# A graph layer on one core: the products of a range's last 32 nodes turned over the four column strips of PE, and a wider spacing of later groups' rank products

## The chip, the cores and the metric

One core of one Trainium2 chip. The metric is the device time of one execution in microseconds. Three runs of the kernel before gave 538.83, 539.52 and 541.97 us; their median is 539.52.

## What is computed

There are 6250 nodes with 128 features and 100,000 edges sorted by destination. Every edge carries one of two messages of its source node, by the edge's type; each node adds up what it receives, adds an own term, and the result goes through relu, a residual and a layer norm.

```python
m_data = X[src] @ W_data.T + b_data
m_ctrl = X[src] @ W_control.T + b_control
msg = where(edge_type == 0, m_data, m_ctrl)
agg = segment_sum(msg, dst, num_segments=6250)
h = x + relu(agg + (x @ W_self.T + b_self))
out = (h - mean(h)) / sqrt(var(h) + 1e-5)
```

## The kernel before

**Tables.** PE first makes both messages of every node, split in three bf16 parts of 128 columns that together hold the fp32 value. They stay in SBUF as m3 (98 tables of 128 rows, 384 columns) and go to DRAM as table.

**Ranges and groups.** 39 ranges of 160 destination nodes (WN) follow, numbered from 0, in 11 groups of 1, 2 and then 4 ranges (GROUPS); group 4 is the fifth and holds ranges 11 to 14. The last few nodes are done at the end of the main part by gathers.

**Ranks.** For each group, `ranks` reads the edges (win), finds each edge's place in a short list by source table, and makes an index. Its steps run over several engines: one-hots of the source block (hots, DVE, L799 and L803), counts (PE, L810) that go out to DRAM and back as past (SP, L830 and L833), rank products (PE, L846, two at a time into the one PSUM buffer rk, each emptied by a DVE reduction to slot, L851), one-hots of the slots (hr and two, DVE, L875 and L881), scatter products (PE, L890), and the write of the result as packed (SP, L917). Edges that find no room in a list go through a second list (L993) and gathered rows gl.

**Sums.** For each range, `sums` loads packed back, broadcast over the partitions, as rows (SP, L1043; three buffers), turns it into a one-hot with a compare on DVE (L1053), and makes a second one-hot hot2 of the destinations in two or three compares (DVE, L1061). Then 25 steps g follow. Stage 1 (L1075) picks messages: four products of 32 output rows, one on each 32-column strip of PE, into a PSUM buffer (g with three buffers, every fourth step x with one). ACT, or DVE where the planner finds it earlier, copies that to SBUF as gs (L484, L485). Stage 2 adds them up by destination in a: four products of 384 columns for the first 128 nodes of the range (L1092), again one on each strip, and three of 128 columns for its last 32 nodes (L1095), one for each of the three bf16 parts, on strips 0, 1 and 2. Stage 2 of a step is put three steps behind stage 1. At the end bs takes the 96 x 128 sums of the last 32 nodes, and a product with fold (L615, a stack of three unit matrices of 32) adds the three parts.

**Order.** Nothing is executed where it is written: `add` hands the planner an instruction, or a list of engines to choose from, with a guessed duration and a due time. `Plan.run` walks through the program in its own time, takes on each engine the ready instruction with the earliest due time, and so writes one fixed order per engine. Due times of the ranks of a group come from the loop at L1191: `when` starts LEAD (80) ahead of the group's ranges, the rank products follow `late` behind it, `step` apart for each table k, and what follows them (scatter, packed, lists) is due behind the last. The planner counts 0.168 us for stage 1 and 0.178 for stage 2.

Of the kernel before, what the change touches and what calls it, by code (L numbers as in the profile page):

```python
# [10 lines left out]
F32 = mybir.dt.float32  # L11
# [5 lines left out]
SP = mybir.EngineType.SP  # L17
# [4 lines left out]
P = 128  # L22
D = 128
D3 = 3 * D
# [20 lines left out]
R = 32  # L45
W4 = WN - P
NT = 2 * NB
NS = 25
# [218 lines left out]
def sums_over_windows(ctx, tc, x, xt, edges, w, bias, out, total):  # L267
    nc = tc.nc
    V, A, G, T, S = nc.vector, nc.scalar, nc.gpsimd, nc.tensor, nc.sync
    dram = ctx.enter_context(tc.tile_pool(name="dram", bufs=1, space=DRAM))  # L270
    const = ctx.enter_context(tc.tile_pool(name="consts", bufs=1))
    work = ctx.enter_context(tc.tile_pool(name="work", bufs=2))
# [3 lines left out]
    add = plan.add  # L276
# [5 lines left out]
    def B(pool, shape, dtype, name, bufs=1, room=None):  # L282
        return Buf(plan, pool, shape, dtype, name, bufs, room)

    def C(shape, dtype, name):
        return Buf(plan, const, shape, dtype, name, 1)

    XC = 4 * WN
    T0 = 36.0
    DOUBLE = ('lo1', 'to1', 'slot2', 'pay', 'inside', 'unit')  # L290
    TW = 13.0
# [4 lines left out]
    AD = 0.45  # L296
    RP, RA, RS = 1, 14, 0.9
    GAP, LEAD, LF, SF = -12, 80, .3, .010


    r0 = C([125, RH, 1], I32, "r0")
# [22 lines left out]
    def vec(due, cols, fn, r, w, rate=1.04):  # L324
        return add("DVE", dve(cols, rate), fn, due, r, w)

    def vp(on_pool, due, cols, fn, r, w, rate=1.04, slow=1.0):
# [15 lines left out]
    ident = C([P, P], F32, "ident")  # L343
# [38 lines left out]
    later = C([P, 2 * R], BF16, "later")  # L382
    vec(2, R, lambda: V.memset(later.t[:, :R], 0.0), [], [(later, 0)], 0.3)
    vec(2, R, lambda: V.memset(later.t[:, R:], 1.0), [], [(later, 1)], 0.3)
    fold = C([3 * R, R], F32, "fold")
    vec(30, R, lambda: V.tensor_add(fold.t, ident.t[: 3 * R, 0:R], ident.t[: 3 * R, R : 2 * R]),
        [ident], [fold])
    vec(30, R, lambda: V.tensor_add(fold.t, fold.t, ident.t[: 3 * R, 2 * R : 3 * R]),
        [ident, fold], [fold])
    minus = C([P, P], BF16, "minus")  # L390
    vec(1.5, P, lambda: V.tensor_scalar_mul(minus.t, ident.t, -1.0), [ident], [minus])
    wbase = C([P, NW], I32, "wbase")
# [28 lines left out]
    def count_rows():  # L421
        for h in range(RH):
# [28 lines left out]
                                    start=True, stop=True), 0.8, [first_f, ident], [first_ps])  # L451
# [6 lines left out]
    def load_edges(b, n, out_, due, buf, key, engine, rows=P):  # L458
        def fn():
# [23 lines left out]
    evict = lambda o, src, cols, due, r, w, lat=0.0: add(  # L483
        [("ACT", act(cols), lambda: A.copy(o(), src())),  # L484
         ("DVE", dve(cols), lambda: V.tensor_copy(o(), src()))], None, None, due, r, w, lat)  # L485
# [14 lines left out]
    m3_key = lambda g: [(m3, (min(g, NS - 1), i)) for i in range(3)]  # L500
# [9 lines left out]
    for c, n in enumerate(XB):  # L510
        cuts = [0, 2, 4, 8, n] if c == 0 else [0, 4, 8, n]
# [15 lines left out]
    for q in range(NS):  # L527
        bs = range(2 * q, min(2 * q + 2, NB))
        nb = len(bs)
        due = 4.0 + MS * q  # L530
# [4 lines left out]
        key = (mp, half)  # L535
        mt = lambda mp=mp, half=half: mp.t[:, half] if len(mp.shape) == 3 else mp.t

        n = 2 * nb * D
        ts = slice(4 * q, 4 * q + 2 * nb)

        for i, b in enumerate(bs):
            c, k, xk = pieces[b]
# [173 lines left out]
    def ranks(gi, w0, nw, when, late, step, engines):  # L716
# [6 lines left out]
        n = nw * KT  # L723
# [62 lines left out]
        vt = low()  # L786
# [7 lines left out]
        for k0 in range(0, KT, ks):  # L794
            k1 = min(k0 + ks, KT)
            m = (k1 - k0) * nw
# [60 lines left out]
        for ci, (k0, k1) in enumerate(zip(cs, cs[1:])):  # L857
            dc = t0 + 1 + step * k1
            m = (k1 - k0) * nw
            c = slice(k0 * nw, k1 * nw)  # L860
            kw = lambda b: b.t.rearrange("p k w -> p (k w)")
            vec(dc, m, lambda c=c, kw=kw: V.tensor_tensor(
                kw(own_n)[:, c], kw(slot)[:, c], kw(unit)[:, c], op=ALU.mult),
                [(slot, k - k % per) for k in range(k0, k1)] + [unit], [(own_n, ci)])
            vec(dc, m, lambda c=c, kw=kw: V.tensor_single_scalar(
                kw(own_n)[:, c], kw(own_n)[:, c], 127, op=ALU.bitwise_and), [(own_n, ci)],
                [(own_n, ci)])
            vec(dc, 2 * m, lambda c=c: V.scalar_tensor_tensor(  # L868
                fl(slot2)[:, c], f2(own_n)[:, c], SLOT0, f2(inside)[:, c], op0=ALU.add,
                op1=ALU.mult), [(own_n, ci), inside], [(slot2, ci)])  # L870
            s4 = [EP, m, R // 2, 2]
            v4 = lambda ap: ap.rearrange("p m (c d) -> p m c d", d=2)
            hr = B(work, [EP, m, R], BF16, "hr", 1, 48 * R)
            two = B(work, [P, m, 2, R], BF16, "two", 1, 48 * 2 * R)
            vec(dc, m * R, lambda c=c, s4=s4, v4=v4, hr=hr: V.tensor_tensor(  # L875
                v4(hr.t),
                slots.t[:EP].rearrange("p (c d) -> p c d", d=2)[:, None].to_broadcast(s4),
                fl(slot2)[:, c, None, :].to_broadcast(s4), op=ALU.is_equal),
                [(slot2, ci), slots], [hr], 0.52)
            for i, f in enumerate((lo1, to1)):  # L880
                tf = lambda e, c=c, s4=s4, v4=v4, i=i, f=f, hr=hr, two=two: e.tensor_tensor(  # L881
                    v4(two.t[:EP, :, i, :]), v4(hr.t),
                    fl(f)[:, c, None, :].to_broadcast(s4), op=ALU.mult)
                vec(dc, m * R, lambda tf=tf: tf(V), [hr, f], [(two, i)], 0.52)

            def scatter(k0=k0, k1=k1, two=two):
                for k in range(k0, k1):
                    for i in range(nw):
                        q = 64 * (i % 2)
                        T.matmul(vv()[q : q + 64, i // 2, :],  # L890
                                 two.t[:EP, (k - k0) * nw + i].rearrange("p f r -> p (f r)"),
                                 ha()[:EP, k, i, :], start=k == 0 and i < 2, stop=k == KT - 1,
                                 skip_group_check=True)
            add("PE", .25 + m * 0.0275, scatter, dc + 1, [(two, 0), (two, 1)] + hkeys(k0, k1), [vt])
        d2 = t0 + 1.5 + step * KT
        vs = B(work, [P, nh, NT], BF16, "vs", 1, 2 * NT)
        both = nw // 2
# [131 lines left out]
        return to_d, gls  # L1029


    def sums(gi, w0, nw, placed):
        to_d, gls = placed
        xc = B(work, [D, nw * WN], F32, "xc", 2, XC)
# [3 lines left out]
        for i in range(nw):  # L1038
# [29 lines left out]
            for g in range(NS):  # L1068
                d = due + TW * g / NS
                gp = B(ps, [P, 512], F32, *(("g", 3) if gi < 2 or g % 4 < 3 else ("x", 1)))  # L1070
                last = g == NS - 1

                def stage1(g=g, gp=gp, sp=sp, last=last):
                    for t in range(2 if last else 4):
                        T.matmul(gp.t[R * t : R * t + R, :D3], sp.t[:, :, 4 * g + t],  # L1075
                                 m3.t[:, 4 * g + t, :], start=True, stop=True)
                s1.append(add("PE", 0.168, stage1, d, [sp] + m3_key(g), [gp]))
                lag = 2 if gi < 2 else 3
                if g >= lag:
                    s2[g - lag].after.append(s1[g])  # L1080
                if last:
                    gs = gls[i]
                    evict(lambda gs=gs: gs.t[:64], lambda gp=gp: gp.t[:64, :D3], D3, d + 0.3,
                          [gp], [(gs, "t")], LAT)
                else:
                    gs = B(work, [P, D3], BF16, "gs", 6)
                    evict(lambda gs=gs: gs.t, lambda gp=gp: gp.t[:, :D3], D3, d + 0.3, [gp], [gs],
                          LAT)

                def stage2(g=g, gs=gs, a=a, hot2=hot2, last=last):  # L1090
                    for j in range(4):
                        T.matmul(a.t[R * j : R * j + R, :D3], hot2.t[:, g, R * j : R * j + R],  # L1092
                                 gs.t, start=g == 0, stop=False, skip_group_check=True)
                    for c in range(3):
                        T.matmul(a.t[R * c : R * c + R, D3:], hot2.t[:, g, P:],  # L1095
                                 gs.t[:, c * D : (c + 1) * D], start=False, stop=last,
                                 skip_group_check=True)
                s2.append(add("PE", 0.178, stage2, d + 0.9, [gs, (hot2, sum(g >= c for c in cuts[1:-1]))], [a]))
                s2[-1].slack = .1
                if g == 12:  # L1100
                    def own_a(i=i, a=a, xc=xc):
                        own(lambda j, m: a.t[R * j : R * j + R, :D],
                            lambda j, m: xc.t[:, i * WN + R * j : i * WN + R * j + R], P)
                    add("PE", 0.28, own_a, d + 1, [xc, w_sb, one3, brows], [a])
            bs = B(work, [3 * R, D], F32, "bs", 5)
            evict(lambda bs=bs: bs.t, lambda a=a: a.t[: 3 * R, D3:], D, due + TW + 0.8, [a], [bs]).slack = 0.25
            got.append((w0 + i, a, due + TW + 0.8, bs))
        return got

# [81 lines left out]
    w0 = 0  # L1191
    todo = []
    for gi, nw in enumerate(GROUPS):
        if gi == 0:
            when, late, step, engines = 0.0, 12.0, 0.5, ["SP"]
        elif gi == 1:
            when, late, step, engines = 8.0, 14.0, 0.6, ["SP", "ACT"]
        else:
            span = nw * TW
            when = max(when + late + 22 * step + GAP, T0 + w0 * TW - LEAD)  # L1200
            late, step, engines = LF * span, SF * span, ["SP"]
        todo.append((gi, w0, nw, when, late, step, engines))
        w0 += nw
    placed = [ranks(*a) for a in todo]
# [169 lines left out]
```

## Time and profile before

| | us |
|---|---|
| median of three runs | 539.52 |
| the profiled execution | 542.22 |
| its span, first to last instruction | 540.4 |
| PE / DVE / ACT / POOL busy | 502.1 / 441.1 / 429.0 / 201.5 |
| first stage 1 product | 60.8 |
| chain of the end: share of PE | 40% |

A row of the timeline has the start, the length, the engine, the line, the operation, what it writes and reads, its size and how many were merged; the idle time ahead of it stands in brackets with what ended it. A row of the groups ends with busy time and mean nanoseconds of one, then the idle time ahead of them. [...] Matmuls of 32 columns each are on one of four strips; the profile doesn't name the strip.

### The profile page before, as it was taken

The numbers are of one execution on the slowest core, as the hardware profiler recorded it, in microseconds if no ns is written. First come the engines' busy times: TensorE is split into PE (matmuls) and PEld (weight loads), VectorE is DVE, ScalarE is ACT, GpSimd is POOL, SyncE is SP. The second block draws the span as 40 slices with busy tenths as digits, with TensorE's granted clock in tenths as the row PEclk, the third lists the DMA queues.
The fourth block names the chain that finished last, engine by engine and source line by source line (L and its number), as shares of the span: only waits on it lengthen the run. The fifth ranks groups of instructions, "written<-read, shape, count | busy, mean of one in ns | idle before, by whom it ended". The sixth has DMA issues, their size and how long they took to land. (4 is left out here: it accounts for less than half of the span.)

```text
span 540.4 us, 30907 instructions
## 1 busy us (share of the span) xinstructions
PE 502.1 (93%) x13288; PEld 432.6 (80%) x13288; DVE 441.1 (82%) x1168; ACT 429.0 (79%) x1077; POOL 201.5 (37%) x284
## 2 busy tenths in 40 slices
PE   7799879799999988999999999999999999999991
PEld 4465557699889877888988887888898899888990
DVE  6388989889989997898989889979978678956642
ACT  4566767698889877888988878978898898878990
POOL 1000535700830684176067247707701720542000
PEclk9989899999999998999999999999999999999997
DMA  7466661540453055325413533351342352234200
GB/s 244 160 256 224 240 181 29 167 161 6 134 145 88 12 139 151 98 77 152 141 38 111 141 95 95 91 180 41 115 128 88 115 163 89 63 107 126 70 19 17
DMA packets 44932, 63.43 MB, mean 117 GB/s; under 512 B 19178, under 2 KB 35279, under 8 KB 44751
## 3 DMA queue, kind: packets, MB, share of 16 engines
q1 hardware_dynamic: 41745, 56.22, 33.5%
q0 software_dynamic: 1120, 2.23, 2.0%
q10 hardware_dynamic: 1922, 2.91, 1.7%
q8 instruction: 106, 1.74, 1.3%
q14 instruction: 39, 0.32, 0.2%
HBM read 45.61 MB, written 13.82 MB: 110 GB/s over the span
## 5 line engine op out<-in xcount | busy, mean ns | idle before, releaser
L1092 PE MATMUL a<-gs,hot 128*32 128x384 bf16 x3744 | 376.1, 328 | 0.4 <-issue 0.3
L484 ACT CAST gs<-g 128x384 bf16<-128x384 f32 x700 | 302.9, 492 | 64.3 <-PE g L1075 53.6
L1075 PE MATMUL g<-m,rows 128*32 128x384 bf16 x2958 | 327.1, 336 | 9.0 <-DVE rows L1053 5.7
L1075 PEld LDWEIGHTS <-rows 128*32 128x32 bf16 x3822 | 253.4, 134 | 27.7 <-DVE rows L1053 6.5
L1095 PE MATMUL a<-gs,hot 128*32 128x128 bf16 x2808 | 273.1, 220 | 2.1 <-issue 2.1
L1092 PEld LDWEIGHTS <-hot 128*32 128x32 bf16 x3900 | 206.4, 98 | 6.7 <-issue 3.1
L1095 PEld LDWEIGHTS <-hot 128*32 128x32 bf16 x2925 | 155.6, 97 | 14.1 <-issue 2.4
L1075 PE MATMUL x<-m,rows 128*32 128x384 bf16 x864 | 122.0, 335 | 0.0
L484 ACT CAST gs<-x 128x384 bf16<-128x384 f32 x199 | 98.3, 494 | 8.6 <-PE x L1075 5.7
L1061 DVE TENSOR_TENSOR hot<-iota_b,to_d 128x1920 bf16<-128x1920 bf16 (+2 forms) x85 | 93.1, 1105 | 0.1
L851 DVE TENSOR_REDUCE slot<-rk 124x8 f32<-124x400 f32 (+2 forms) x99 | 56.1, 567 | 22.3 <-PE g L1075 10.3
L674 POOL TENSOR_SCALAR xr<-xr,mv,rstd 128x128 f32<-128x128 f32 (+1 forms) x44 | 56.5, 1289 | 21.9 <-DVE rstd L651 18.4
L846 PE MATMUL rk<-hots,tri 128*32 128x400 bf16 (+1 forms) x388 | 51.3, 337 | 4.5 <-DVE slot L851 1.5
L1053 DVE TENSOR_SCALAR rows<-rows,pid 128x3136 bf16<-128x3136 bf16 (+1 forms) x46 | 41.6, 904 | 5.7 <-DMA rows<-packed 5.7
L937 POOL TENSOR_SCALAR pv<-slot 124x88 f32<-124x88 bf16 x9 | 9.5, 1058 | 79.6 <-DVE slot L868 74.2
L624 DVE TENSOR_REDUCE s<-a 128x128 f32<-128x384 f32 (+1 forms) x40 | 22.1, 551 | 15.7 <-ACT bs L484 9.9
L1016 POOL DMA_INDIRECT sr<-table,at x20 | 29.8, 1489 | 10.8 <-DVE at L1004 6.2
L491 POOL COPY to_d<-vs 32x100 bf16<-32x100 bf16 (+1 forms) x72 | 29.2, 406 | 5.9 <-DVE vs L911 2.7
L846 PEld LDWEIGHTS <-tri 128*32 128x32 bf16 x428 | 22.9, 96 | 9.9 <-issue 8.6
L803 DVE TENSOR_TENSOR hots<-hots,val 124x1200 bf16<-124x1200 bf16 (+3 forms) x42 | 28.0, 675 | 0.0
L799 DVE TENSOR_TENSOR hots<-iota_b,st 124x1200 bf16<-124x1200 bf16 (+3 forms) x42 | 27.6, 671 | 0.0
L767 POOL TENSOR_SCALAR pay<-u 124x88 f32<-124x88 f32 x9 | 8.9, 994 | 46.2 <-DVE u L752 45.1
(224 smaller groups left out, 667.9 us busy)
## 6 DMA issues: line engine op xcount, KB each, us to landing
rows<-packed SPq DMA_DIRECT2D x36, 784.0 KB
table<-m SPq DMA_DIRECT2D x12, 768.0 KB
xc<-in_xt SPq DMA_DIRECT2D x9, 320.0 KB
rows<-packed ACTq DMA_DIRECT2D x3, 784.0 KB
rows<-in_xt SPq DMA_DIRECT2D x8, 256.0 KB
xr<-in_x SPq DMA_DIRECT2D x8, 256.0 KB
out<-xr SPq DMA_DIRECT2D x8, 256.0 KB
gl<-sr SPq DMA_DIRECT2D x39, 48.0 KB
```

The source lines that it names most:

```text
L484: [("ACT", act(cols), lambda: A.copy(o(), src())), ("DVE", dve(cols), lambda: V.tensor_copy(o(), src()))], None, None, due, r, w, lat)
L491: "POOL", 0.25 + cols * 0.0014, lambda: G.tensor_copy(o(), src()), due, r, w)
L674: fp = lambda k=k, m=m: G.tensor_scalar(h.t[:m, k, :], h.t[:m, k, :], mv.t[:m, k, 0:1], rstd.t[:m, k : k + 1], op0=ALU.subtract, op1=ALU.mult)
L803: vec(when + 2 + pace * k0, m * NC, lambda k0=k0, k1=k1, hs4=hs4, hp=hp: V.tensor_tensor(hp(), hp(), fl(val)[:, k0 * nw : k1 * nw, None, : ...
L846: T.matmul(acc.t[R * j : R * j + R, : (k1 - k0) * wide], tri.t[:, R * j : R * j + R], flat(k0, k1, P), start=True, stop=True, skip_group_c ...
L851: vec(due, (k1 - k0) * wide, lambda k0=k0, k1=k1, acc=acc: V.tensor_reduce(slot.t[:, k0:k1, :], acc.t[:EP, : (k1 - k0) * wide].rearrange(" ...
L1016: add("POOL", GC, lambda pr=pr, sr=sr: G.indirect_dma_start(out=sr.t[: room(pr)], out_offset=None, in_=table[:, :], in_offset=bass.Indirec ...
L1053: add("DVE", dve(half * NT, 0.305) + 0.05, lambda sp=sp, rs=rs: V.tensor_scalar(sp.t[:, rs], sp.t[:, rs], pid1.t, None, op0=ALU.is_equal), ...
L1061: lambda i=i, hot2=hot2, s4=s4, c0=c0, c1=c1: V.tensor_tensor(hot2.t[:, c0:c1].rearrange("p g (c d) -> p g c d", d=2), iota1_b.t.rearrange ...
L1075: T.matmul(gp.t[R * t : R * t + R, :D3], sp.t[:, :, 4 * g + t], m3.t[:, 4 * g + t, :], start=True, stop=True)
L1092: T.matmul(a.t[R * j : R * j + R, :D3], hot2.t[:, g, R * j : R * j + R], gs.t, start=g == 0, stop=False, skip_group_check=True)
L1095: T.matmul(a.t[R * c : R * c + R, D3:], hot2.t[:, g, P:], gs.t[:, c * D : (c + 1) * D], start=False, stop=last, skip_group_check=True)
```

## The change

```diff
+    LEAD4, SF4 = 90, .025
...
-    fold = C([3 * R, R], F32, "fold")
-    vec(30, R, lambda: V.tensor_add(fold.t, ident.t[: 3 * R, 0:R], ident.t[: 3 * R, R : 2 * R]),
+    fold = C([P, R], F32, "fold")
+    vec(30, R, lambda: V.tensor_add(fold.t, ident.t[:, 0:R], ident.t[:, R : 2 * R]),
...
+    for j in (2, 3):
+        vec(30, R, lambda j=j: V.tensor_add(fold.t, fold.t, ident.t[:, R * j : R * j + R]),
...
-            add("PE", .25 + m * 0.0275, scatter, dc + 1, [(two, 0), (two, 1)] + hkeys(k0, k1), [vt])
+            add("PE", .2 + m * 0.016, scatter, dc + 1, [(two, 0), (two, 1)] + hkeys(k0, k1), [vt])
...
+    load = [0] * 4
+
+    def turn(n, cols):
+
+        js = sorted(range(4), key=lambda j: (load[j], j))[:n]
+        for j in js:
+            load[j] += cols
+        return js
...
-                    for t in range(2 if last else 4):
+                    for t in (0, 1) if last else turn(4, D3):
...
-                s1.append(add("PE", 0.168, stage1, d, [sp] + m3_key(g), [gp]))
+                s1.append(add("PE", 0.163, stage1, d, [sp] + m3_key(g), [gp]))
...
-                    for j in range(4):
+                    for j in turn(4, D3):
...
-                    for c in range(3):
-                        T.matmul(a.t[R * c : R * c + R, D3:], hot2.t[:, g, P:],
-                                 gs.t[:, c * D : (c + 1) * D], start=False, stop=last,
+                    for c, j in enumerate(turn(3, D)):
+                        T.matmul(a.t[R * j : R * j + R, D3:], hot2.t[:, g, P:],
+                                 gs.t[:, c * D : (c + 1) * D], start=False, stop=g > NS - 3,
...
-                s2.append(add("PE", 0.178, stage2, d + 0.9, [gs, (hot2, sum(g >= c for c in cuts[1:-1]))], [a]))
+                s2.append(add("PE", 0.204, stage2, d + 0.9, [gs, (hot2, sum(g >= c for c in cuts[1:-1]))], [a]))
...
-            bs = B(work, [3 * R, D], F32, "bs", 5)
-            evict(lambda bs=bs: bs.t, lambda a=a: a.t[: 3 * R, D3:], D, due + TW + 0.8, [a], [bs]).slack = 0.25
+            bs = B(work, [P, D], F32, "bs", 5)
+            evict(lambda bs=bs: bs.t, lambda a=a: a.t[:, D3:], D, due + TW + 0.8, [a], [bs]).slack = 0.25
...
-            when = max(when + late + 22 * step + GAP, T0 + w0 * TW - LEAD)
-            late, step, engines = LF * span, SF * span, ["SP"]
+            when = max(when + late + 22 * step + GAP, T0 + w0 * TW - (LEAD if gi < 4 else LEAD4))
+            late, step, engines = LF * span, (SF if gi < 4 else SF4) * span, ["SP"]
```

`turn` keeps a count of columns for each strip. The three products for the last 32 nodes go to the three strips with the smallest count, and every set of four products begins with the strip that has the least. The sums of the last 32 nodes then lie on all four strips, so bs has 128 rows and fold is a stack of four unit matrices. The planner now counts 0.163 and 0.204 us for the two stages, less for scatter products, and for group 4 on the rank phase starts 10 earlier, with rank products due 1.3 apart for each table instead of 0.52.

New line numbers are up to 11 higher than the old ones. Two places of the orders show what moves. The first is SP's queue around the load of range 11, the first of group 4: packed is this group's write, win are loads of edges, past is the write for the group after, the two rows are the loads for ranges 11 and 12. Before:

```order
L917 DMA packed<-vs 128x2x98
L462 TENSOR_LOAD first
L468 ISA
L468 DMA win<-in_edges 124x66
L830 DMA past<-csb 64x2x200
L462 TENSOR_LOAD first
L468 ISA
L468 DMA win<-in_edges 124x66
L1043 DMA rows<-packed 128x3136 x2
```

and now, where the first rows is the load for range 10:

```order
L1046 DMA xc<-in_xt 128x640
L599 DMA xr<-in_x 128x4x128
L606 DMA xr<-in_x 32x128 x4
L1054 DMA rows<-packed 128x3136
L919 DMA packed<-vs 128x2x98
L1054 DMA rows<-packed 128x3136
L609 DMA xb<-in_xt 128x4x32
```

The load for range 11 now stands right behind packed; the two win loads and the past write no longer come between.

The second is DVE ahead of the first hot compare of range 9 (the last row of each; hot_4899 before, hot_5188 now). Before, group 4's reductions are still under way there:

```order
L1053 TENSOR_SCALAR rows<-rows,pid_129 128x3136
L851 TENSOR_REDUCE slot<-rk 124x8
L803 TENSOR_TENSOR hots<-hots,val 124x1200
L799 TENSOR_TENSOR hots<-iota_b,st_4141 124x1200
L851 TENSOR_REDUCE slot<-rk 124x8
L803 TENSOR_TENSOR hots<-hots,val 124x1200
L624 TENSOR_REDUCE s<-a 128x128
L851 TENSOR_REDUCE slot<-rk 124x8
L1061 TENSOR_TENSOR hot_4899<-iota_b,to_d 128x2080
```

and now its one-hots of slots are behind it:

```order
L870 SCALAR_TENSOR_TENSOR slot_4573<-own_n,inside 124x80
L487 CAST gs<-g 128x384
L877 TENSOR_TENSOR hr<-slot_f,slot_4573 124x1280
L1028 TENSOR_REDUCE smax<-slot_4573 124x1
L883 TENSOR_TENSOR two<-hr,lo_3433 124x40x32
L883 TENSOR_TENSOR two<-hr,to_2479 124x40x32
L947 MAX m_624<-pv 124x8 x4
L805 TENSOR_TENSOR hots<-hots,val 124x1200
L1072 TENSOR_TENSOR hot_5188<-iota_b,to_d 128x2080
```

Counted from the start of the program, six more reductions L851, two more hr and four more two now stand ahead of this compare.

More of the change, by code (lines that the diff above doesn't have):

```diff
@@ L384, in sums_over_windows @@
     vec(2, R, lambda: V.memset(later.t[:, R:], 1.0), [], [(later, 1)], 0.3)
-    fold = C([3 * R, R], F32, "fold")
-    vec(30, R, lambda: V.tensor_add(fold.t, ident.t[: 3 * R, 0:R], ident.t[: 3 * R, R : 2 * R]),
+    fold = C([P, R], F32, "fold")
+    vec(30, R, lambda: V.tensor_add(fold.t, ident.t[:, 0:R], ident.t[:, R : 2 * R]),
         [ident], [fold])
-    vec(30, R, lambda: V.tensor_add(fold.t, fold.t, ident.t[: 3 * R, 2 * R : 3 * R]),
-        [ident, fold], [fold])
+    for j in (2, 3):
+        vec(30, R, lambda j=j: V.tensor_add(fold.t, fold.t, ident.t[:, R * j : R * j + R]),
+            [ident, fold], [fold])
     minus = C([P, P], BF16, "minus")
```

## The prediction

> **What bounds the kernel now.** I read the page first, then the busy times by stretch, PE's timeline inside one range, ACT's timeline, and the waits where PE fell idle.
>
> ```profile
> span 540.4 us, 30907 instructions
> PE 502.1 (93%) x13288; PEld 432.6 (80%) x13288; DVE 441.1 (82%) x1168; ACT 429.0 (79%) x1077; POOL 201.5 (37%) x284
> ```
>
> PE is busy for 93% of the span, but "busy" there means that at least one of its four column strips works. What counts is the load of the fullest strip, so I looked at the starts inside a stretch without other work:
>
> ```profile
> 249.90 0.39 PE L1092 MATMUL a<-gs,hot 128*32 128x384 bf16 x4
> 250.06 0.22 PE L1095 MATMUL a<-gs,hot 128*32 128x128 bf16 x1
> 250.08 0.38 PE L1075 MATMUL g<-m,rows 128*32 128x384 bf16 x1
> 250.08 0.22 PE L1095 MATMUL a<-gs,hot 128*32 128x128 bf16 x1
> 250.12 0.33 PE L1075 MATMUL g<-m,rows 128*32 128x384 bf16 x1
> 250.12 0.22 PE L1095 MATMUL a<-gs,hot 128*32 128x128 bf16 x1
> ...
> 250.28 0.39 PE L1092 MATMUL a<-gs,hot 128*32 128x384 bf16 x4
> ...
> 250.66 0.39 PE L1092 MATMUL a<-gs,hot 128*32 128x384 bf16 x4
> ```
>
> L1092 comes round every 0.38 us: that is one step g. Follow strip 0: a 384-column product at 249.90, the 128-column product of L1095 at 250.06 (0.16 us later), stage 1 of L1075 at 250.12 (0.06 later), L1092 again at 250.28 (0.16 later). So 0.16 + 0.06 + 0.16 us of one strip's columns make the whole step. Strip 3 gets no L1095 product: one L1075 starts at 250.08, ahead of the last L1095 at 250.12, which the program issues before it. The strips run apart from each other, and strip 3 has the 0.06 us to spare.
>
> By stretch (group borders; columns PE, PEld, DVE, ACT, POOL busy, clock, DMA):
>
> ```profile
> core 0: us, PE busy (x) PEld busy (x) DVE busy (x) ACT busy (x) POOL busy (x), PEclk, DMA share, GB/s
> 60.80:105.60 44.80, 38.99 (x1045) 32.05 (x1046) 41.12 (x123) 32.68 (x82) 23.44 (x32) 0.96 0.45 133
> 105.60:153.90 48.30, 46.33 (x1343) 42.24 (x1339) 44.36 (x117) 40.15 (x104) 18.58 (x31) 1.00 0.34 98
> 174.80:203.80 29.00, 25.77 (x775) 22.61 (x767) 28.14 (x77) 21.88 (x57) 20.99 (x32) 1.00 0.32 79
> 203.80:252.00 48.20, 46.74 (x1315) 40.27 (x1317) 40.97 (x98) 39.43 (x100) 25.23 (x34) 0.96 0.38 108
> 485.40:526.00 40.60, 39.90 (x1165) 37.41 (x1161) 23.47 (x53) 36.33 (x94) 3.92 (x5) 1.00 0.25 71
> ```
>
> Up to 203.8 us (ranges 0 to 10) DVE is 92 to 97% busy in the stretches shown and PE has holes: there DVE sets the pace. From 203.8 to 526 PE does 28 ranges in 322.2 us, 11.5 us each, of which 25 x 0.38 = 9.5 us is the strip chain and the rest own terms, rank, scatter and list products and waits. There PE's strips bound the time.
>
> **The change, part by part.** *Strips.* Per step the columns are 4 x 384 + 4 x 384 + 3 x 128 = 3456. Before, strips 0 to 2 carry 896 and strip 3 768; with the turn each carries 864. At 0.38 us for 896 columns the 32 columns are 13.6 ns. By how the traced strips run apart, reordering inside a step costs nothing. Over all 39 x 25 = 975 steps that is 13.2 us; over the 28 ranges where PE bounds, 700 x 13.6 = 9.5 us. [...]
>
> What is late next is ACT, which empties g:
>
> ```profile
> 254.78 0.48 ACT L484 CAST gs<-x 128x384 bf16<-128x384 f32 x1
> 255.15 1.26 ACT L484 CAST gs<-g 128x384 bf16<-128x384 f32 x3
> 256.26 0.53 ACT L484 CAST gs<-x 128x384 bf16<-128x384 f32 x1
> 256.63 1.31 ACT L484 CAST gs<-g 128x384 bf16<-128x384 f32 x3
> 257.74 0.58 ACT L484 CAST gs<-x 128x384 bf16<-128x384 f32 x1
> ```
>
> The x buffer takes every fourth step, and its casts start at 254.78, 256.26 and 257.74: four casts in 1.48 us, 0.371 each, with no idle between. So where PE has only steps to do, the step falls from 0.38 to 0.371, not 0.366: 700 x 9 ns = 6.3 us is the lower end. Other PE work in a range (2 of the 11.5 us) lets ACT catch up through four buffers. I take 6.7 us of 6.3 to 9.5; for ranges 0 to 10 I take nothing, at most 275 x 13.6 ns = 3.7.
>
> *Order: rank products, due times, costs.* One wait stands out:
>
> ```profile
> PE g L1075 <- DVE rows L1053: 3.2, 1, 3.2
> 204.80:208.00 3.20, 2.95 (x46) 2.22 (x49) 2.52 (x5) 1.73 (x5) 2.73 (x3) 0.50 0.91 294
> 189.37 0.40 SPq L917 DMA_DIRECT2D packed<-vs  x1
> 190.46 0.28 SPq L468 DMA_DIRECT2D win<-in_edges  x1
> 193.36 0.66 SPq L830 DMA_DIRECT2D past<-csb  x1
> 195.12 0.30 SPq L468 DMA_DIRECT2D win<-in_edges  x1
> 195.52 1.91 SPq L1043 DMA_DIRECT2D rows<-packed  x2
> 202.74 1.03 DVE L1053 TENSOR_SCALAR rows<-rows,pid 128x3136 bf16<-128x3136 bf16 x1
> ```
>
> PE stands still for 3.2 us until the rows compare of range 11 (the first of the fifth group) ends at 203.77, and then runs at a granted clock of 0.50 for 3.2 us, which is another 1.6. The rows load was issued at 195.52, 6.2 us behind packed, because a win load and the past write of the next group stood between on SP. In the new order the rows load stands right behind packed, and packed itself comes earlier: counting stage 1 products in the two orders, this group's last scatter product stands behind 9.98 ranges of them before and 8.69 now. All of 4.8 us can go. Upper end: the two ranges from 174.8 to 200.6 took 12.9 us each against 11.5 later, 2.8 more, so 7.6. Lower end 0, if DVE is late for another reason (below). I take 4.3.
>
> *Nothing, with cover.* fold gains one 128x32 add in the start-up, under 0.1 us of DVE. The fold product contracts over 128 partitions in place of 96 and the bs copy reads 128, both with the same columns; ACT's 21% idle time covers them. The counts of casts in the two orders go from 42 to 24 on DVE, the rest moves to ACT:
>
> ```profile
> L485 DVE CAST gs<-g 128x384 bf16<-128x384 f32 x17 | 9.3, 549 | 4.0 <-PE g L1075 3.9
> ```
>
> That frees 18 x 0.55 = 9.9 us on DVE and costs ACT 18 x 0.371 = 6.7 us of its 111 idle; if ACT had no idle time left it would cost those 6.7. The win loads come earlier on SP, where the words ahead show room; without it, a rows load would slip by their 0.3 us each.
>
> Sum: 6.7 + 4.3 = 11.0. The profiled execution took 542.22 us (span 540.4), so 531.2 on its scale. It lies 2.7 above the median of the runs, 539.52; on that scale 528.5.
>
> **Rivals.** *DVE keeps the pace.* If DVE has no reserve up to about 350 us, faster strips only wait more: the steps gain nothing and of the stall 3 us remain as a gain, 536.5. For it: 92 to 97% busy up to 203.8. Against: the casts that leave DVE, and 7.2 us idle in 203.8 to 252.
>
> *Slower: one-hot compares behind rank work.* In the new order two more one-hot blocks and six more reductions of group 4 stand ahead of the first hot compare of range 9:
>
> ```profile
> 167.73 1.23 DVE L1061 TENSOR_TENSOR hot<-iota_b,to_d 128x2080 bf16<-128x2080 bf16 x1
> L1075 PEld LDWEIGHTS <-rows x882: 131/133/162, 60.8 to 174.7; 128*32 128x32 bf16 x177
> L851 DVE TENSOR_REDUCE slot<-rk 124x8 f32<-124x400 f32 x88 | 50.1, 569 | 19.9 <-PE g L1075 9.8 <-PE rk L846 7.0 <-PE x L1075 2.4
> L875 DVE TENSOR_TENSOR hr<-slot_f,slot 124x1536 bf16<-124x1536 bf16 (+1 forms) x16 | 14.5, 904 | 0.4
> L881 DVE TENSOR_TENSOR two<-hr,to 124x1536 bf16<-124x1536 bf16 (+1 forms) x16 | 15.8, 985 | 0.0
> L881 DVE TENSOR_TENSOR two<-hr,lo 124x1536 bf16<-124x1536 bf16 (+1 forms) x16 | 14.1, 880 | 0.0
> ```
>
> That is 6 x 0.569 + 2 x 0.904 + 2 x 0.985 + 2 x 0.880 = 9.0 us. The compare ended at 168.96 and PE reached range 9 (after 9 x 98 = 882 weight loads) just behind 174.7, so 5.8 us of slack are exceeded by 3.2. It decides once DVE cannot win back those 3.2 us from its 3.9 idle between 105.6 and 153.9. Those reductions also waited 19.9 us for PE, which spacing the products out may give back or not. If the loss recurs in four groups, 12.8 us are lost against 4.8 of the stall and some 4.3 of steps (19 ranges x 25 x 9 ns): 3.7 net, 543.2.
>
> *Strip 3 is not free.* One L1075 of four took 0.38 against 0.33 above. If it is held up by the others rather than idle, evening out gains nothing and only the order does: 535.2. Against: that product started 0.04 us ahead of its neighbours, and it is not in the chain that makes the 0.38.
>
> *All of it.* 13.2 + 7.6 us, 518.7, if ACT keeps up and DVE's early ranges follow.
>
> **How the numbers follow.** A measurement here can tell some 0.5%, 2.7 us, from no change. Forecast 0.55 (524 to 532); DVE keeps the pace 0.17; strip 3 not free 0.10; all of it 0.10; slower 0.08. Faster by over 0.5% (below 536.8) is 0.55 + 0.10 + 0.10 and 0.05 of the DVE case, 0.80; same 0.12, the rest of that case; slower 0.08. The range 521 to 538 holds the forecast, the two middle cases and the near half of "all of it", and leaves out the slower case.
>
> **What would show it.** Right: L1092 comes round every 0.37 us in stretches without other work; no idle of PE in front of range 11 and no clock of 0.50 behind it; ACT's casts back to back. Wrong: steps still at 0.38; a PE wait for the hot compares near range 9; DVE above 95% past 204 us.

## The result, and the profile after

The changed kernel took 548.72 us (546.55 to 550.23, four runs) beside 539.71 for the kernel before (538.83 to 541.97, four runs): ratio 1.0134, 95% interval 1.0088 to 1.0181. It is 9 us slower. Some executions of a kernel run over 1.5% above its fastest: a time below is the median of all, while ratios, and the profiled executions read here, leave those out. The profiled execution took 549.98 us. From its page:

```profile
span 548.4 us, 30928 instructions
PE 498.2 (91%) x13288; PEld 426.9 (78%) x13288; DVE 431.1 (79%) x1154; ACT 432.4 (79%) x1092; POOL 210.3 (38%) x284
```

PE is busy 4 us less than before, DVE 10 us less and ACT 3 us more, all in the direction forecast. The span is 8 us longer all the same, so the time went into idle. The stretches that answer to the first four shown of before, with ranges 7 and 8 in the third row and range 20 in the last:

```profile
core 0: us, PE busy (x) PEld busy (x) DVE busy (x) ACT busy (x) POOL busy (x), PEclk, DMA share, GB/s
60.60:111.10 50.50, 42.85 (x1056) 33.66 (x1060) 43.47 (x128) 32.93 (x83) 20.56 (x31) 0.87 0.38 114
111.10:157.10 46.00, 45.11 (x1363) 41.31 (x1359) 43.33 (x113) 40.95 (x107) 18.14 (x28) 1.00 0.33 102
157.10:181.30 24.20, 23.11 (x723) 21.02 (x719) 22.39 (x54) 19.77 (x52) 5.21 (x8) 1.00 0.34 106
181.30:204.80 23.50, 22.49 (x634) 19.28 (x629) 20.67 (x50) 20.13 (x55) 21.53 (x24) 1.00 0.41 110
204.80:253.40 48.60, 45.33 (x1352) 40.67 (x1347) 43.91 (x108) 39.68 (x103) 26.83 (x34) 1.00 0.35 106
313.00:329.50 16.50, 13.07 (x399) 11.33 (x392) 12.27 (x39) 10.55 (x29) 11.53 (x21) 1.00 0.20 65
```

Row 1 holds ranges 0 to 2: 50.5 us where before had 44.8, at a clock of 0.87. Row 4 holds ranges 9 and 10: 23.5 against 29.0; 3.2 of that is the stall in front of range 11, which is gone. These 5.5 us and the 2.3 of ranges 3 to 6 (row 2, 46.0 against 48.3) are eaten by the start and by ranges 7 and 8 (24.2 against 20.9), and range 11 begins at 204.8 us (before: 203.8). From there to the last range's end it is 330.8 us against 323.4, where the forecast had a gain of 6.7.

PE's weight loads show what kind of idle it is. From the list of their waits, the longest first, of the changed kernel:

```profile
engine line waited for: us in total, times, longest us
PEld L1103 <- issue: 14.1, 19, 2.0
PEld L1086 <- issue: 8.6, 19, 1.5
PEld L1106 <- issue: 7.9, 9, 2.0
```

and of the kernel before:

```profile
...
PEld L1075 <- issue: 6.1, 11, 1.7
...
PEld L1092 <- issue: 3.1, 11, 0.6
...
PEld L1095 <- issue: 2.4, 4, 0.6
```

"issue" is time in which the engine waited for nothing that the profile shows. Over the three weight loads of a step it was 11.6 us before and is 30.6 now. Below, **issue idle** always means the sum of these three rows in a kernel's profiled execution. One of these places, PE around 357.5 us, in range 23 (start, length; the idle ahead in brackets):

```profile
357.53 0.14 PEld L1086 LDWEIGHTS <-rows 128*32 128x32 bf16 x3
359.67 0.10 PEld L1103 LDWEIGHTS <-hot 128*32 128x32 bf16 x4 [2.00 <-issue]
```

On SP shortly before, and what the DMA queues moved from 352.5 to 357.5 us:

```profile
352.44 0.36 SPq L1054 DMA_DIRECT2D rows<-packed  x1
352.89 0.40 SPq L599 DMA_DIRECT2D xr<-in_x  x1
353.34 1.89 SPq L606 DMA_DIRECT2D xr<-in_x  x4
355.27 0.42 SPq L1046 DMA_DIRECT2D xc<-in_xt  x1
```

```profile
DMA packets 912, 1.31 MB, mean 262 GB/s; under 512 B 89, under 2 KB 716, under 8 KB 911
...
q1 hardware_dynamic: 911, 1.30, 82.9%
q8 instruction: 1, 0.02, 1.2%
```

A queue of its own, q8, moves instructions, 106 packets in the whole run, all of 16,384 bytes:

```profile
q8 instruction: 106, 1.74, 1.3%
```

PE has 2 x 13288 = 26,576 matmuls and weight loads, 251 for each packet. The page doesn't say whose instructions the packets hold. Single records of the trace: packets began at 349.99 and then only at 357.41 us, 7.42 apart where 4 is usual, and took 0.96; PE went on at 359.67. This suggested that PE ran out of instructions while loads were in the way. The trace's 90 intervals between such packets from 105 to 515 us, by what the data queues had moved in the 4 us ahead:

| moved in 4 us | intervals | mean us | over 5.5 us |
|---|---|---|---|
| under 500 KB | 56 | 4.00 | 3 |
| 500 to 950 KB | 18 | 4.72 | 4 |
| over 950 KB | 16 | 6.34 | 10 |

One load of rows is 784 KB; with an xr or out of 256 KB or an xc of 320 KB right behind it the top class is reached. The packets could also be late because PE was, and not PE because of them, so the table alone decides nothing.

What PE did right behind the packets decides it. Between 105 and 519 us of the changed kernel there are eleven times at which PE started neither a product nor a weight load for over 0.9 us and waited for nothing that the profile shows. Each time it went on 1.24 to 1.53 us behind the end of a packet of q8. So I take it that PE stood without instructions until the packet came; had the loads only slowed PE's own reading, nothing would tie its stops to the ends of these packets. The same holds for every such stop in e10, e12, e14 and e15 below (1.24 to 1.64 us). A late packet alone doesn't stop PE: 17 of the 90 intervals here are over 5.5 us, but so are 16 of 91 in the kernel before and 18 of 92 in e1. The difference is in the longest: 13 are over 6.5 us here, where the kernel before has 4 and e1 has 5, and ten of the 13 end in a stop of over 0.37 us.

### The profile page after: what moved, and what is told of

It reads as the page before. It is cut to its first block, busy times and chain, and to the rows that moved or that the text cites. A ratio compares the mean times of both kernels' runs of the same rounds, so it can differ in the third digit from the quotient of the medians.

```text
span 548.4 us, 30928 instructions
## 1 busy us (share of the span) xinstructions
PE 498.2 (91%) x13288; PEld 426.9 (78%) x13288; DVE 431.1 (79%) x1154; ACT 432.4 (79%) x1092; POOL 210.3 (38%) x284
## 5 line engine op out<-in xcount | busy, mean ns | idle before, releaser
L1103 PE MATMUL a<-gs,hot 128*32 128x384 bf16 x3744 | 358.6, 329 | 7.0 <-issue 6.7
L1086 PE MATMUL g<-m,rows 128*32 128x384 bf16 x2958 | 298.5, 336 | 9.0 <-issue 2.3
L1086 PEld LDWEIGHTS <-rows 128*32 128x32 bf16 x3822 | 268.6, 135 | 23.1 <-issue 8.6
L1106 PE MATMUL a<-gs,hot 128*32 128x128 bf16 x2808 | 275.2, 220 | 5.4 <-issue 5.3
L1103 PEld LDWEIGHTS <-hot 128*32 128x32 bf16 x3900 | 177.0, 98 | 19.7 <-issue 14.1
L1106 PEld LDWEIGHTS <-hot 128*32 128x32 bf16 x2925 | 157.4, 97 | 19.1 <-issue 7.9
L486 ACT CAST gs<-x 128x384 bf16<-128x384 f32 x211 | 107.9, 511 | 17.8 <-PE x L1086 10.2
L1086 PE MATMUL x<-m,rows 128*32 128x384 bf16 x864 | 92.6, 331 | 1.6 <-issue 1.4
L676 POOL TENSOR_SCALAR xr<-xr,mv,rstd 128x128 f32<-128x128 f32 (+1 forms) x44 | 62.5, 1428 | 31.6 <-DVE rstd L653 30.1
L848 PE MATMUL rk<-hots,tri 128*32 128x400 bf16 (+1 forms) x388 | 39.0, 335 | 3.8 <-DVE slot L853 1.3
L493 POOL COPY to_d<-vs 32x100 bf16<-32x100 bf16 (+1 forms) x72 | 34.5, 480 | 10.3 <-DMA t_msg<-table,t_idx 3.2
L848 PEld LDWEIGHTS <-tri 128*32 128x32 bf16 x428 | 19.3, 97 | 9.5 <-issue 7.6
```

Of the source, the lines that this page charges most:

```text
L486: [("ACT", act(cols), lambda: A.copy(o(), src())), ("DVE", dve(cols), lambda: V.tensor_copy(o(), src()))], None, None, due, r, w, lat)
L493: "POOL", 0.25 + cols * 0.0014, lambda: G.tensor_copy(o(), src()), due, r, w)
L676: fp = lambda k=k, m=m: G.tensor_scalar(h.t[:m, k, :], h.t[:m, k, :], mv.t[:m, k, 0:1], rstd.t[:m, k : k + 1], op0=ALU.subtract, op1=ALU.mult)
L848: T.matmul(acc.t[R * j : R * j + R, : (k1 - k0) * wide], tri.t[:, R * j : R * j + R], flat(k0, k1, P), start=True, stop=True, skip_group_c ...
L1106: T.matmul(a.t[R * j : R * j + R, D3:], hot2.t[:, g, P:], gs.t[:, c * D : (c + 1) * D], start=False, stop=g > NS - 3, skip_group_check=True)
```

## The experiments

Ratios are to the kernel before on the same chip, with the 95% interval; the kernel before took 536.85 to 540.75 us beside them (medians), so ratios and not times are compared between rows. The last column is the issue idle; a dash stands where there is none to read.

| kernel | us | ratio | issue idle |
|---|---|---|---|
| changed kernel | 548.72 | 1.0134 (1.0088 to 1.0181) | 30.6 |
| e1 turn | 534.71 | 0.9882 (0.9837 to 0.9926) | 12.6 |
| e2 costs | 545.75 | 1.0093 (1.0060 to 1.0126) | 22.6 |
| e3 due times | 538.26 | 0.9986 (0.9959 to 1.0013) | 9.3 |
| e4 casts to DVE | 541.90 | 1.0012 (0.9979 to 1.0045) | 11.3 |
| e5 the same and turn | 536.63 | 0.9931 (0.9891 to 0.9971) | 15.8 |
| e6 turn, due times | 534.47 | 0.9900 (0.9863 to 0.9937) | 14.0 |
| e7 turn, costs | 537.91 | 0.9930 (0.9886 to 0.9973) | - |
| e8 turn, stage costs | 550.18 | 1.0198 (1.0138 to 1.0258) | 18.3 |
| e10 turn, 256 KB more | 542.72 | 1.0096 (1.0063 to 1.0128) | 16.3 |
| e12 changed, half of rows | 528.69 | 0.9827 (0.9768 to 0.9886) | 12.7 |
| e13 turn, half of rows | 525.95 | 0.9807 (0.9767 to 0.9847) | 4.0 |
| e14 changed, 0.206 | 536.39 | 0.9998 (0.9971 to 1.0024) | 17.7 |
| e17 changed, 0.202 | 541.21 | 1.0051 (1.0010 to 1.0093) | 20.1 |
| e15 changed, rows in halves | 557.11 | 1.0345 (1.0262 to 1.0428) | 29.6 |
| e16 turn, rows in halves | 570.21 | 1.0572 (1.0478 to 1.0665) | - |
| e18 before, 0.180 | 550.23 | 1.0247 (1.0181 to 1.0313) | 10.7 |
| e20 before, 0.176 | 543.49 | 1.0055 (1.0020 to 1.0090) | 11.6 |
| e19 e18 with turn | 550.15 | 1.0193 (1.0117 to 1.0268) | 23.4 |

Issue idle alone doesn't rank the kernels: e18 has 10.7 at a ratio of 1.0247, e17 20.1 at 1.0051.

**The parts alone.** e1 is the kernel before with `turn`, the wide bs and the wide fold; its order is that of the kernel before on every engine. Expected:

> Only the turn over the strips with its wider bs and fold; planner costs and due times as before, so the order on every engine is that of before. Theory A (the copies out of g on ACT end 0.382 us apart at best, which is as slow as the strip chain was): steps stay at 0.38 us and the time within 2.5 us of before. Rival B (strip 3 is held up by the others and never was idle): also no change here, told apart by the next two runs. Rival C (the turn itself costs PE something): slower by 3 us or more. My forecast's first term would be 6.7 us faster.

Theory A fell: 6 us faster. The turn does what the forecast's term for the strips said. e2 has the new costs only:

```diff
-                s1.append(add("PE", 0.168, stage1, d, [sp] + m3_key(g), [gp]))
+                s1.append(add("PE", 0.163, stage1, d, [sp] + m3_key(g), [gp]))
-                s2.append(add("PE", 0.178, stage2, d + 0.9, [gs, (hot2, sum(g >= c for c in cuts[1:-1]))], [a]))
+                s2.append(add("PE", 0.204, stage2, d + 0.9, [gs, (hot2, sum(g >= c for c in cuts[1:-1]))], [a]))
-            add("PE", .25 + m * 0.0275, scatter, dc + 1, [(two, 0), (two, 1)] + hkeys(k0, k1), [vt])
+            add("PE", .2 + m * 0.016, scatter, dc + 1, [(two, 0), (two, 1)] + hkeys(k0, k1), [vt])
```

> Only the planner's costs: 0.163 and 0.204 us for the two stages and the smaller scatter cost; strips and due times of ranks as before. Theory A: the planner believes PE slower and leaves more copies on ACT; if that and the new order are what costs, this run takes most of the 9 us, 545 to 549. Rival D (the due times of groups 4 on are at fault): this run within 3 us of before, and the loss appears in a run with the due times alone.

5 us slower, as theory A had it. e3 has LEAD4 and SF4 only, e6 these with the turn, e7 the turn with e2's costs:

> Only the due times of the ranks of groups 4 on (90 ahead, 1.3 apart); strips and planner costs as before. What is known so far: the turn alone 6 us faster, the costs alone 5 us slower, all together 9 us slower. Theory E (the parts add up): this run is some 10 us slower than before, 548 to 552, with the loss behind range 11. Rival F (only the due times and the costs together make the bad order): within 3 us of before.

> The turn and the due times, planner costs as before. Theory E: 6 less than the run with the due times alone, 542 to 546. Rival F: as the turn alone, 533 to 537.

> The turn and the planner costs, due times as before. Theory E: minus 6 plus 5, so 538 to 541. Rival G (the costs fit PE's real pace only with the turn, and then the order is good): faster than the turn alone, below 533.

The due times cost nothing, alone or with the turn: theory E fell, and rival F held. The turn with the costs gains 3.8 by its ratio, more than theory E's sum and less than rival G. No sum of parts gives 1.0134. e8 leaves only the scatter cost of e7 at the old value:

> The turn with the two stage costs alone (0.163 and 0.204), the scatter cost and the due times as before. Theory H (the stage costs make the loss of the costs, by 18 copies more on ACT and a later order at the start): as the run with all costs, 538 to 541, with range 0 some 3 us longer than before. Rival I (the scatter cost does it): as the turn alone, 533 to 537.

It is by far the worst of these, 2% slower, outside both ranges: a smaller change than e7 costs more. That spoke against any price per part, and for the order itself as the cause.

**Casts.** e4 and e5 send every third cast of ranges 35 to 38 to DVE, without and with the turn, to see whether ACT's casts set the step there:

```diff
-                    evict(lambda gs=gs: gs.t, lambda gp=gp: gp.t[:, :D3], D3, d + 0.3, [gp], [gs],
+                    (dvecopy if gi > 9 and g % 3 == 1 else evict)(
+                          lambda gs=gs: gs.t, lambda gp=gp: gp.t[:, :D3], D3, d + 0.3, [gp], [gs],
```

> Kernel before, with every third copy out of g forced onto DVE in the last four ranges (35 to 38), where DVE is little used; strips as before. Theory A and B alike: the strips bound here too, steps of ranges 36 to 38 stay at 0.38 us although ACT now has a third less to do; whole time within 1.5 us of before.

> The run above with the turn over the strips, in the same order. Theory A: with a third of the copies off ACT the steps of ranges 36 to 38 fall to 0.367 us (864 columns in place of 896), some 1.0 us over the three ranges against the run without the turn. Rival B: they stay at 0.38.

They told nothing apart: the planner laid the forced casts out unevenly, and ranges 36 and 37 took 10.7 and 10.0 us in e4 against 9.81 before.

**Bytes and the fetch.** e10 keeps e1's order on every engine and puts one more load right behind each load of rows:

```diff
+                    if gi > 3:
+                        S.dma_start(more[i % 2].t, xt[:, i * 512 : i * 512 + 512])
```

> The turn alone again (534.7 us beside 540.8), in the same order on every engine, but from the fifth group on each load of rows (784 KB) has a load of 256 KB of node features right behind it on SP, into a tile that nothing reads. Theory J: the slow steps of the changed kernel at which TensorE's next instruction waits for nothing are TensorE's instruction fetch, held up when the data queues move 1 MB and more in 4 us; so the steps that are late without a wait, 4.2 us from range 11 on in the turn alone, rise to 9 or more, and the whole goes to 539 to 550 us. Rival K: the late steps come with the order of the instructions, not with the bytes; then 533 to 537 us and 3 to 6 us of late steps.

542.7: bytes that nobody uses cost 2.1 points, 11 us. e12 and e13 keep the order too and halve the rows loads from the fifth group on, and so leave out part of the sums:

```diff
+                RL = R if gi < 4 else R // 2
...
+                    sp.t[:, :RL].rearrange("p r c -> p (r c)"),
+                    packed[gi, i // 2, (i % 2) * 64 : (i % 2) * 64 + RL, :]
+                    .rearrange("r c -> (r c)")[None, :].to_broadcast([P, RL * NT])),
...
+                rs = slice(q * half, (q + 1) * half) if gi < 4 else slice(0, RL)
...
+                            sp.t[:, :RL].rearrange("p r (h c) -> p (r h) c", h=2)
+                            [:, :, (4 * g + t) % NB]),
```

> The changed kernel with its order kept on every engine, but from the fifth group on a load of rows brings 392 KB instead of 784 (half of the rows; the compare works on that half, 0.5 us shorter, and the products take their 32 columns from it, so the sums aren't the reference's). Theory J: the late steps without a wait, 15.1 us from range 11 on, fall below 7, and the whole from 548.7 to 541 or less. Rival K: 12 to 18 us of late steps stay, and the time is 546 to 550.

> The same halved load of rows (and so the same part of the sums left out) in the turn alone, in its own order. Theory J: little is late there (4.2 us), so 530 to 534.5 us: a smaller gain than in the changed kernel. Rival K: 533 to 536, as the turn alone.

e12 is 3.1 points below the changed kernel, some 16 us, with the same order; e13 only 0.8 below e1, 4 us. e12's issue rows, from the list of its waits:

```profile
...
PEld L1087 <- issue: 6.2, 12, 1.5
...
PEld L1107 <- issue: 4.4, 5, 1.5
...
PEld L1110 <- issue: 2.1, 2, 1.4
```

The rows stand for L1086, L1103 and L1106 of the changed kernel: 12.7 us where that had 30.6. Counted as the expectations count them (steps at which the next instruction has no wait, late by over 0.35 us, from range 11 on), it is 15.1 us in the changed kernel and 3.6 in e12, 4.2 in e1, 13.5 in e10, none in e13. (In e10 the issue idle of the table rises less, from 12.6 to 16.3.) (e13's 525.95 us lies below the 530 expected. Its chip was a fast one: the kernel before took 536.85 there, beside 540.75 in e1's runs, and on that scale e13 is at 529.8.) Theory J held in all three: with the order fixed, the bytes of the loads move this idle, and the time follows. A half load also halves the columns of the compare (0.40 us less as an estimate: in the changed kernel 3136 columns take 1.02 us and 1568 take 0.62) and eases DVE; that part isn't separated, but the rows with "issue" don't depend on it.

**The order.** e14 and e17 move one cost of the changed kernel by a hundredth, e18 and e20 one of the kernel before:

```diff
-                s2.append(add("PE", 0.204, stage2, d + 0.9, [gs, (hot2, sum(g >= c for c in cuts[1:-1]))], [a]))
+                s2.append(add("PE", 0.206, stage2, d + 0.9, [gs, (hot2, sum(g >= c for c in cuts[1:-1]))], [a]))
```

This is e14; in e17 the new number is 0.202, in e18 0.180 for 0.178, and in e20 0.176.

> The changed kernel with one planner number moved by a hundredth (a step's second products booked at 0.206 us instead of 0.204): the order moves at many places, for no reason that the chip knows. Theory L: the 14 us are a matter of which loads and steps happen to meet in this one order; then this kernel lies anywhere from 533 to 550 us, and off the changed kernel by over 3 us. Rival M: they belong to the new costs and due times as such; then 546 to 551.

> The changed kernel with a step's second products booked at 0.202 us instead of 0.204, once more an order moved for no reason. Theory L (the changed kernel's order is a bad draw): 533 to 545 us. Rival M (the costs and due times as such cost most of the 14 us, and the jog to 0.206 was a lucky draw): 546 to 551.

> The kernel before with one planner number moved by a hundredth (a step's second products booked at 0.180 us instead of 0.178), nothing else. Theory L: orders of this kernel differ by several us for no reason, so its ratio to the kernel before is off 1 by over 0.005 with 6 chances in 10, to either side (533 to 549 us). Rival N (the order before is typical, and a small jog does nothing): within 0.003, 538 to 541.

> The kernel before with a step's second products booked at 0.176 us instead of 0.178, a third draw of its order. Theory L: off the kernel before by over 0.005 with 6 chances in 10, and slower rather than faster, as the order before is the best of those seen with these strips. Rival N: within 0.003.

Theory L held in all four, though e18's 550.23 us lies just above its range and e20's interval (1.0020 to 1.0090) reaches below the 1.005. The changed kernel loses its whole excess when 0.204 becomes 0.206, and three fifths of it with 0.202: rival M is out. The kernel before gets 2.5% slower from 0.178 to 0.180. There the loss has another cause than the fetch; its waits from 320 to 347 us, in range 21, which took 24.5 us instead of 12.3 in the kernel before:

```profile
POOL unit L754 <- DVE own_n L862: 11.7, 1, 11.7
ACT bs L484 <- PE vt L615: 8.6, 1, 8.6
PEld L890 <- DVE two L881: 4.6, 1, 4.6
...
PE vt L615 <- DVE vs L911: 2.8, 1, 2.8
```

In that order a group's scatter products (L890) and the fold product (L615) stand in PE's queue ahead of steps whose data is there, and PE waits 4.6 and 2.8 us for DVE. The clock granted from 322.0 to 346.5 us is 0.79, where the kernel before has 1.00 in that range; as an estimate, 0.21 of 24.5 is another 5.1 us, and the three come to 12.5, about the 12.2 lost. So one draw of the order can lose in the fetch, another in a queue.

**Is it the burst?** e15 and e16 cut each rows load in two of 392 KB, 4 us apart in time:

```diff
-    RP, RA, RS = 1, 14, 0.9
+    RP, RA, RS = 2, 14, 4.0
```

> The changed kernel with each load of rows cut in two of 392 KB, the second due 4 us behind the first; the sums stay whole, and the planner draws a new order throughout. Theory J (the burst, not the sum of the bytes, holds the fetch up): under 7 us of late steps without a wait, and 530 to 537 us. Theory L (each new order is a draw, and the bytes are the same): 533 to 550 us, with 7 to 15 us of such steps.

> The turn alone with the same halves of the rows load. Theory J: 0 to 4 us of late steps without a wait and 529 to 534 us, the best of the kernels whose sums are whole. Theory L: 530 to 542, with 4 to 12 us of them.

Theory J in this sharper form fell: both are much slower (e15's late steps come to 17.2 us), and slower than theory L's 550 and 542 us too. In e15 17 of 37 intervals between packets of q8 are over 5.5 us already in the class from 500 to 950 KB, where the changed kernel has 4 of 18. So cutting the loads didn't keep the packets on time. The order is a new one as well, so how much of the loss is fetch (in e16 0.069 of the ratio beside e1) stays open.

**The turn in another order.** e19 has e1's turn and e18's 0.180, and its order is that of e18:

> The turn over the strips, put into the kernel before with the 0.180 jog (which took 550.2 us beside 537.6), and nothing else; the order of every engine is that of the jogged kernel. If the turn's gain is its own, and the order's price another term that adds to it, the ratio is 1.0247 less 0.012: 1.008 to 1.018, 542 to 547 us. If the turn alone was faster only because of the places where that order's loads met its steps, the ratio is anywhere from 0.995 to 1.03.

The ratio fell by 0.005, with overlapping intervals: less than the 0.012 expected, just outside 1.008 to 1.018, and no proof of a gain. The hole in range 21 is there again (24.7 us); the issue idle went from 10.7 to 23.4. Range 37, where little else runs, still went from 9.81 to 9.51 us. So the turn's gain per step is there, and in this order the rest was lost elsewhere. e1, e5, e6, e7 and e19 each keep the order of a kernel without the turn (before, e4, e3, e2 and e18): the ratio falls by 0.012, 0.008, 0.009, 0.016 and 0.005, 0.010 or 5.4 us on average.

## Why the prediction was wrong, point by point

*Strips, 6.7 us: right in size.* e1 gave 6.0 us (540.75 to 534.71). In the profiled executions all of it comes from range 11 on, as forecast: 316.9 us there against 323.4, and 143.3 against 143.0 in ranges 0 to 10. In ranges 36 and 37 the gain was 9.81 to 9.50 and 9.52 us, 12 ns a step where 13.6 were forecast. Rival "strip 3 is not free" is out. So is "DVE keeps the pace", by which steps up to about 350 us gain nothing: ranges 11 to 22 took 140.3 us in e1 and 142.6 before. One reason in it was misread. I took 0.371 us a cast from the starts of ACT's casts. In the quoted rows the casts of x end at 254.78 + 0.48 = 255.26 and 256.26 + 0.53 = 256.79, 1.53 us for four, 0.382 each, and the changed kernel shows the same:

```profile
519.11 0.53 ACT L486 CAST gs<-x 128x384 bf16<-128x384 f32 x1
...
520.59 0.58 ACT L486 CAST gs<-x 128x384 bf16<-128x384 f32 x1
```

Starts creep ahead while lengths grow (0.48, 0.53, 0.58), so the ends count. What "would show it", rounds of 0.37 us, didn't come: PE's rounds in the last ranges of the changed kernel are still 0.38, the same as the ends of ACT's casts beside them, which follow each other without idle; so it seems that ACT holds them there.

```profile
519.30 0.35 PE L1103 MATMUL a<-gs,hot 128*32 128x384 bf16 x4
...
519.68 0.35 PE L1103 MATMUL a<-gs,hot 128*32 128x384 bf16 x4
...
520.07 0.35 PE L1103 MATMUL a<-gs,hot 128*32 128x384 bf16 x4
...
520.45 0.35 PE L1103 MATMUL a<-gs,hot 128*32 128x384 bf16 x4
```

Then the gain comes from steps in which PE has own terms or other products to do besides. That would explain how a wrong cadence gave a fair size, partly by luck; the split wasn't tested.

*The stall of range 11, 4.3 us: went as forecast, and more was lost.* The compare of range 11's rows ends at 200.58, PE needs it at 204.8:

```profile
199.57 1.01 DVE L1064 TENSOR_SCALAR rows<-rows,pid 128x3136 bf16<-128x3136 bf16 x1
```

Ranges 9 and 10 are 5.5 us shorter, and the clock granted behind them, from 204.8 to 253.4 us, is 1.00 (before: 0.96). Rival "one-hot compares behind rank work" is out: its first hot compare ends at 178.64 us, and PE reaches range 9 at 181.3.

*Casts and win loads at nothing: right for what they are.* 26 casts are left on DVE (24 were counted in the forecast); ACT is busy 3 us more, within its idle. The fold product took 273 ns over 96 partitions and over 128, a copy to bs on ACT 284 ns in place of 263, and the add for fold 0.18 us where under 0.1 was forecast.

*The step that failed* is the order term, 4.3 us with a "lower end 0": it priced a new order by the one wait that I saw in the old one. The new costs and due times drew a new order for the whole program, and that order loses in places where the old one lost nothing: from range 11 on 13.9 us against e1 (330.8 and 316.9). Most of that, as I read the stops, is PE without instructions: the late steps without a wait come to 15.1 us there against 4.2 in e1, and with half of the rows' bytes in the same order (e12) to 3.6. Another part is range 20: 16.5 us (13.6 before), where POOL waits 3.2 us for a gather (t_msg) that stands ahead of its copies, and PE and DVE behind it:

```profile
DVE hr L976 <- POOL pos L970: 3.9, 1, 3.9
...
POOL to_d L493 <- DMA t_msg<-table,t_idx: 3.2, 1, 3.2
...
PEld L995 <- DVE hr L976: 2.0, 1, 2.0
...
PE a L1192 <- DMA t_msg<-table,t_idx: 1.6, 1, 1.6
```

*The range and the chances.* Six orders with the strips of before (before, e2, e3, e4, e18, e20) lie from 0.9986 to 1.0247, mean 1.0066; nine with the turn (the changed kernel, e1, e5, e6, e7, e8, e14, e17, e19) from 0.9882 to 1.0198, mean 1.0024, standard deviation 0.0125, which is 7 us. So the kernel before stands on a good order, the other five with its strips are 0.8% slower on average, and a change of the order costs some 4 us before it gains anything, give or take 7. Beside that, a gain of 11 us with 8 in 100 for slower was far too sure. The starting loss of ranges 0 to 2 (50.5 us against 44.8) is not shown to be the order's alone: e1, e4, e5, e10 and e13 have the order of before there, and their profiled executions took 47.5, 47.7, 47.7, 48.8 and 44.7 us; e12, with the changed kernel's order, took 49.3. The granted clock is part of it: 0.87 against 0.96, as an estimate 0.13 x 50.5 - 0.04 x 44.8 = 4.8 us.

## What to carry to other kernels

If a planner writes one fixed order from guessed costs, a change of costs or due times is a new draw of that order; price the draw (here 7 us either way) by jogging one number by a hundredth before believing in a gain or loss of that size. Test the arithmetic of a change with the order held fixed: e1 showed 6 us in one run that the full change hid behind 14. And rows with "issue" on the engine that bounds the time are worth a look at the instruction queue: half the bytes of the rows loads (and part of the sums left out) gave 4 to 16 us here without a single instruction moved.

## What the runs showed of the hardware

Instructions arrive during the run, in 106 packets of 16 KB on the DMA queue q8, and in the changed kernel these came later when more data moved: 4.0 us between packets with less than 500 KB moved in 4 us, 6.3 with over 950 KB. Eleven times PE stood there for 0.96 to 2.08 us, behind intervals of 5.69 to 9.71 us between packets and until 1.24 to 1.53 us behind the end of the late one. 256 KB more behind each rows load cost 11 us (e10), half of each rows load gave 4 and 16 (e13, e12). Back-to-back casts of 384 columns from PSUM end 0.38 us apart on ACT in the kernel before and the changed one, though in the quoted rows their starts stand 0.371 apart. Around two holes in PE's work the granted clock was low: 0.50 for 3.2 us behind the stall of range 11 before, 0.79 over range 21 in e18.

No kernel whose sums are whole was faster than the turn alone (0.9882 of the kernel before; 0.9900 with the due times).
